# Spreading 500 samples of an edge list over the partitions: by a matmul from the list in SBUF in place of a DMA of single words

## The chip, the cores and the metric

The kernel runs on one core of a Trainium2 chip. The metric is the device time of one execution in microseconds (us), and the median of three runs is given. Beside it there is one profiled execution, from which all views of the trace are taken. Engines are named as the profile names them: PE (TensorE), DVE (VectorE), ACT (ScalarE), POOL (GpSimd) and SP (SyncE). A "q" behind the name (ACTq, SPq) marks what an engine's sequencer does, such as issuing a DMA.

## The reference

A graph has 3,125 nodes with 128 features each and 100,000 edges. The edge list is given as `src`, `dst` and `edge_type_8` (0 to 7), sorted by `dst`. Four graph layers follow one another; each adds its result to its input, and a layer norm follows. Cut to what matters:

```
edge_index = stack([src, dst])
x = layernorm(x + L0(x, ..., src, dst))             # three GCN layers, weights by degree, self loops
x = layernorm(x + L1(x, edge_index, W, b))          # sum over the neighbours and the node itself
x = layernorm(x + L2(x, edge_index, eps, ...))      # GIN: sum over neighbours, two linear layers with batch norm
x = layernorm(x + L3(x, edge_index, edge_type_8, ...))   # two relational layers, a mean per relation
```

Every layer needs the adjacency of the graph, which the kernel has to make out of the edge list first.

## The kernel before, in words

The function `listed` does the work (a second function, `general`, is there for graphs that don't fit the first one's limits, and does not run here). It has three parts.

**From the edge list to matrices.** The three lists are loaded as tiles of 125 partitions by 800 words (L171). Two arrays go back to DRAM from them: `dsf`, which is the target list as floats in rows of 200 (written at L182, made by the cast at L181), and `pk`, in which target, type and source of an edge are packed in one word (written at L189, made by two DVE operations at L184 and L186; L190 writes a short tail of -1 behind it). Then each half block of 64 nodes needs the place where its edges begin. `search(s)` finds it for two half blocks at a time, for 128 slots in parallel. First it counts how many of 500 samples of the target list, every 200th edge, lie below the node's number (L213); the samples must lie in every partition for that (`smb`). The count gives the row of `dsf` that an indirect DMA of POOL fetches (`g`, L220); counting in that row (L225) gives the exact place, `ptr`. `keys(s)` fetches the edges from there out of `pk` (`ew`, L235), unpacks them, transposes them on PE and leaves them in `kT`. `total(b)` makes one-hot matrices of them on DVE (L162), multiplies them on PE (L272) to a 128-row slab of the adjacency, and writes the slab and its transpose to DRAM. These calls are made for `s` from 0 to 12, two calls of `search` ahead.

**The layers L0 to L2** multiply with the adjacency slabs. Between their matmuls the generator `relations()` makes matrices for the eight relations.

**The relational layers L3** multiply with these, and gather the edges of the last blocks by indirect DMAs of POOL.

How the 500 samples come to lie in every partition is the subject of this document. `smp` is loaded by a DMA on ACT's queue that takes every 200th word of `dst` in DRAM (L174); `smf` is its cast to float on DVE (L179); a matmul with a row of ones (L193) spreads the row over 128 partitions in PSUM, and ACT copies it to `smb` (L195):

```python
nc.scalar.dma_start(smp, p["dst"].rearrange("(o i j) -> o i j", o=1, j=200)[:, :, 0])
...
nc.tensor.matmul(t[:, :500], ones[0:1, :], smf, start=True, stop=True)
```

What is issued in which order is not the order of the source. A scheduler places each engine's instructions by what they depend on, and moves loads that depend on nothing to the front. So ACT's queue also holds, near the start, the load of the node features `xa` (L473, 24 blocks of 128 rows, and L476, the last 53 rows) and eight loads of bias and scale columns by `column` (L95), which only layers L2 and L3 use. DMAs from SP and ACT report their end on eight semaphores, which the scheduler hands out in turn: the ninth DMA waits, before it is issued, for the end of the first, and so on. In the built program the waits of the start stand as follows. The column loads are the tenth to the seventeenth of these DMAs. On ACT the order is `smp`, `xa`, a load of the activation table, the copy to `smb`, the rest of `xa`, and then the eight column loads, which wait in turn for `e_dst`, `xa`, `e_src`, `e_edge_type`, `dsf`, `pk<-none`, the rest of `xa`, and `pk<-w`. On SP the order is `e_dst`, `e_src`, `e_edge_type`, `dsf`, `pk<-none`, `pk<-w`. On DVE it is some memsets, `smf`, `df`, `w`, `w` with the target, two copies for `iota50`, `identb`, and then the first counts of `search(0)`.

Of the kernel before, what the change touches and what calls it, by code (L numbers as in the profile page):

```python
# [8 lines left out]
F32 = mybir.dt.float32  # L9
BF = mybir.dt.bfloat16  # L10
I32 = mybir.dt.int32
# [4 lines left out]
OP = mybir.AluOpType  # L16
# [14 lines left out]
EP = 125  # L31
# [14 lines left out]
def cols(m0, nb):  # L46
    return slice(m0 * P, (m0 + nb) * P)
# [25 lines left out]
def listed(ctx: ExitStack, tc: tile.TileContext, p: dict, out: bass.AP, bad):  # L73


    nc = tc.nc
# [4 lines left out]
    ident = const.tile([P, P], F32, name="ident")  # L81
# [5 lines left out]
    ones = const.tile([P, P], F32, name="ones")  # L87
# [60 lines left out]
    with tc.tile_pool(name="f_bg", bufs=1) as bg, tc.tile_pool(  # L148
        name="f_ps", bufs=1, space=PSUM
# [17 lines left out]
        with tc.tile_pool(name="f_t1", bufs=1) as t1:  # L167

            ei = [t1.tile([EP, ET], I32, name=f"e_{n}") for n in ("dst", "src", "edge_type_8")]
            for t, name in zip(ei, ("dst", "src", "edge_type_8")):  # L170
                nc.sync.dma_start(t, p[name].rearrange("(p t) -> p t", p=EP))  # L171
            smp = t1.tile([1, 500], I32, name="smp")
            with nc.allow_non_contiguous_dma(reason="every 200th edge"):
                nc.scalar.dma_start(smp, p["dst"].rearrange("(o i j) -> o i j", o=1, j=200)[:, :, 0])  # L174
            nid = t1.tile([P, NC2], F32, name="nid")
            nc.gpsimd.iota(nid, pattern=[[2 * P, SB], [1, 2]], base=0, channel_multiplier=2,
                           allow_small_or_imprecise_dtypes=True)
            smf = t1.tile([1, 500], F32, name="smf")
            nc.vector.tensor_copy(smf, smp)  # L179
            df = t1.tile([EP, ET], F32, name="df")  # L180
            nc.vector.tensor_copy(df, ei[0])  # L181
            nc.sync.dma_start(dsf.rearrange("(p a) c -> p (a c)", p=EP), df)  # L182
            w = t1.tile([EP, ET], I32, name="w0")
            nc.vector.scalar_tensor_tensor(w, ei[2], 12, ei[1], op0=OP.logical_shift_left, op1=OP.bitwise_or)  # L184
            w2 = t1.tile([EP, ET], I32, name="w1")
# [4 lines left out]
            nc.sync.dma_start(pk[E:].rearrange("(o t) c -> o (t c)", o=GM), none)  # L190

            t = psum.tile([P, 512], F32, name="mi", tag="mi", bufs=2)
            nc.tensor.matmul(t[:, :500], ones[0:1, :], smf, start=True, stop=True)  # L193
            smb = t1.tile([P, 500], F32, name="smb")
            nc.scalar.copy(smb, t[:, :500])  # L195

# [110 lines left out]
            for g in range(2):  # L307
                t = psum.tile([P, 512], F32, name="mi", tag="mi", bufs=2)
                rs = t1.tile([P, 512], F32, name="rs", bufs=2)
                nc.vector.memset(rs, 0.0)  # L310
                for i in range(4 * g, min(7, 4 * g + 4)):
                    q, w = 32 * (i % 4), min(512, NP - 512 * i)
# [19 lines left out]
            t = psum.tile([P, 512], F32, name="mi", tag="mi", bufs=2)  # L332
# [5 lines left out]
            t = psum.tile([P, 512], F32, name="mi", tag="mi", bufs=2)  # L338
# [132 lines left out]
        with tc.tile_pool(name="f_nd", bufs=1) as nd:  # L471
# [127 lines left out]
            t = psum.tile([P, 512], F32, name="mi", tag="mi", bufs=2)  # L599
# [69 lines left out]
            for m0, nb in CH:  # L669
                t = psum.tile([P, 512], F32, name="bld", tag="bld", bufs=2)  # L670
                for i in range(nb):
                    o = t[:, cols(i, 1)]
# [8 lines left out]
    with tc.tile_pool(name="f_rel", bufs=1) as rp, tc.tile_pool(  # L681
        name="f_psr", bufs=1, space=PSUM
# [175 lines left out]
        with tc.tile_pool(name="f_hr", bufs=1) as hp:  # L858
# [15 lines left out]
            for m0, nb in CH:  # L874
                o = psum.tile([P, 512], F32, name="mi", tag="mi", bufs=2)
                for a in range(2):
                    nc.tensor.matmul(o[:, : nb * P], root2[:, a, :], hT[:, a, cols(m0, nb)],
                                     start=(a == 0), stop=(a == 1))
# [623 lines left out]
@with_exitstack  # L1502
def gnn_kernel(ctx: ExitStack, tc: tile.TileContext, p: dict, out: bass.AP):
    bad = ctx.enter_context(tc.tile_pool(name="flag", bufs=1)).tile([P, 1], I32, name="bad")
    listed(tc, p, out, bad)
    rv = tc.nc.values_load(bad[0:1, 0:1], min_val=0, max_val=1)  # L1506
    with tc.If(rv > 0):
        general(tc, p, out)
# [32 lines left out]
```

## Time and profile before

| | |
|---|---|
| median of 3 runs | 2260.39 us (2258.17 to 2264.78) |
| the profiled execution's own time | 2260.0 us |
| its span, first to last instruction | 2258.2 us |
| mean granted TensorE clock | 0.938 of full speed |
| PE busy, DVE busy, POOL busy, ACT busy | 1955.4, 1376.9, 954.5, 791.5 us |
| DMA, mean over the span | 192 GB/s |
| first 30 us: PE, DVE, ACT busy | 2.03, 7.59, 2.02 us |
| 30 to 58 us: PE, DVE busy | 9.42, 22.05 us |
| 58 to 263 us (adjacency slabs): PE, DVE busy | 138.39, 175.09 us |
| 330 to 960 us (L0 to L2): PE busy | 624.17 us of 630 |

The span leaves out 1.8 us of the execution's own time. The rows of the table with a stretch of time are answers of the trace for that stretch: in the first 30 us no engine is busy for more than a quarter of the time, so it is waits that set its length; after that DVE, and later PE, carry the kernel.

### The profile page before, as it was taken

The page shows a single profiled execution, that of the slowest core. Times are in us where ns is not written, and L with a number is a line of the kernel's source. Part 1 is how long each engine was busy: PE and PEld are TensorE (multiplying, and loading weights), DVE is VectorE, ACT ScalarE, POOL GpSimd, SP SyncE. Part 2 cuts the span into 40 slices and gives each one's busy share as a digit, 9 for nine tenths or more (in the row PEclk, how much of TensorE's full clock was granted, in tenths as well). Part 3 has the DMA queues.
Part 4 walks back from the last instruction along what each step waited for, and adds up shares of the span by engine and source line. Part 5 has one row for each costly group of instructions (what it writes and reads, how often), then busy time and mean ns, then how long its engine had stood idle before and what let it go on. Part 6 is the DMA issues. An engine that isn't in the chain of part 4 may idle for free. (4 is left out here: it accounts for less than half of the span.)

```text
span 2258.2 us, 32584 instructions
## 1 busy us (share of the span) xinstructions
PE 1955.4 (87%) x12551; PEld 1351.3 (60%) x12551; DVE 1376.9 (61%) x2385; ACT 791.5 (35%) x1027; POOL 954.5 (42%) x898
## 2 busy tenths in 40 slices
PE   1666669999999999957999999999878998899894
PEld 1444436666665555445668667758745776777772
DVE  4888889999996430045435345435337776666663
ACT  1666734545442110044223233233224333232230
POOL 3222121211210000002757547727723887777875
PEclk9777779999999999978999999999989999999996
DMA  3444476887888666427657467637637887788762
GB/s 93 176 189 166 178 193 211 287 284 257 272 277 269 180 193 177 120 60 222 173 140 212 139 185 213 187 117 207 172 99 219 241 238 221 201 229 228 199 172 77
DMA packets 384638, 433.10 MB, mean 192 GB/s; under 512 B 28731, under 2 KB 350301, under 8 KB 384472
## 3 DMA queue, kind: packets, MB, share of 16 engines
q1 hardware_dynamic: 314318, 278.95, 40.7%
q0 software_dynamic: 45920, 119.66, 18.2%
q10 hardware_dynamic: 24234, 32.31, 5.0%
q8 instruction: 100, 1.64, 0.3%
q14 instruction: 66, 0.54, 0.1%
HBM read 319.22 MB, written 111.58 MB: 191 GB/s over the span
## 5 line engine op out<-in xcount | busy, mean ns | idle before, releaser
L738 PE MATMUL acc<-m,hilo 128*128 128x384 f32 (+1 forms) x3200 | 758.5, 383 | 12.0 <-DVE m L735 6.6
L772 POOL DMA_INDIRECT gx<-xt_d,gsrc x355 | 393.6, 1109 | 573.2 <-DMA m<-rel 357.2
L738 PEld LDWEIGHTS acc<-m,hilo 128*128 128x128 f32 x3200 | 577.6, 193 | 80.3 <-issue 8.9
L539 PE MATMUL acc<-m,parts 128*128 128x512 bf16 (+1 forms) x2625 | 539.3, 357 | 15.7 <-issue 12.7
L772 POOL DMA_INDIRECT gx<-ht_d,gsrc x355 | 412.9, 1163 | 167.0 <-issue 56.4
L733 ACT CAST m<-m 128x1920 fp32r<-128x1920 uint8 (+1 forms) x128 | 264.2, 2064 | 540.1 <-PE acc L738 491.5
L735 DVE CAST m<-m 128x2560 fp32r<-128x2560 uint8 (+1 forms) x192 | 302.6, 1576 | 161.3 <-PE acc L738 92.5
L539 PEld LDWEIGHTS <-parts 128*128 128x128 bf16 x2625 | 255.3, 98 | 238.3 <-issue 17.9
L780 PE MATMUL ga<-oh,gx 128*128 128x192 bf16 (+1 forms) x2442 | 273.5, 246 | 98.8 <-DMA gx<-ht_d,gsrc 57.7
L780 PEld LDWEIGHTS <-gx 128*128 128x128 bf16 x2442 | 170.7, 99 | 206.9 <-DMA gx<-ht_d,gsrc 83.1
L456 ACT CAST rb<-bld 128x800 uint16<-128x800 f32 x179 | 143.9, 828 | 129.7 <-PE bld L449 121.4
L463 POOL DMA_DIRECT2D rel<-rb x112 | 64.3, 582 | 287.5 <-ACT rb L456 162.6
L764 DVE TENSOR_TENSOR oh<-iota,gkey 128x768 bf16<-128x768 bf16 (+1 forms) x188 | 99.5, 530 | 92.2 <-PE ga L780 89.2
L162 DVE TENSOR_TENSOR lo<-iota,kT 128x2048 bf16<-128x2048 bf16 x100 | 122.0, 1220 | 0.0
L712 DVE TENSOR_TENSOR e<-mi,t 128x512 f32<-128x512 f32 x50 | 34.3, 688 | 133.8 <-ACT t L711 133.8
L272 PE MATMUL bld<-hi,lo 128*128 128x50 bf16 x1600 | 74.4, 200 | 46.1 <-DVE hi L162 38.9
L449 PE MATMUL bld<-rhq,rlo 128*128 128x200 bf16 x896 | 107.6, 252 | 1.8 <-DVE rb L458 1.1
L272 PEld LDWEIGHTS <-lo 128*128 128x128 bf16 x1600 | 63.4, 107 | 70.6 <-DVE hi L162 26.3
L449 PEld LDWEIGHTS <-rlo 128*128 128x128 bf16 x896 | 82.4, 98 | 36.7 <-issue 9.0
L162 DVE TENSOR_TENSOR rhq<-iota,kT 128x3200 bf16<-128x3200 bf16 x56 | 102.2, 1824 | 0.0
L828 PE MATMUL mi<-wr,hT 128*128 128x512 f32 x200 | 93.9, 604 | 4.8 <-DVE e L712 4.7
L285 ACT ACTIVATE av<-mi 128x896 bf16<-128x896 bf16 (+1 forms) x100 | 82.8, 835 | 31.4 <-PE mi L284 30.1
(212 smaller groups left out, 1813.4 us busy)
## 6 DMA issues: line engine op xcount, KB each, us to landing
m<-rel SPq DMA_DIRECT2D x160, 320.0 KB, 4.1
rel<-rb POOLq DMA_DIRECT2D x112, 400.0 KB, 6.5
m<-adj SPq DMA_DIRECT2D x60, 640.0 KB, 7.3
m<-rel SPq DMA_DIRECT2D x160, 240.0 KB, 3.2
m<-adj_t SPq DMA_DIRECT2D x40, 640.0 KB, 4.1
m<-adj SPq DMA_DIRECT2D x45, 480.0 KB, 6.1
adj_t<-at SPq DMA_DIRECT2D x25, 800.0 KB
adj<-av SPq DMA_DIRECT2D x25, 800.0 KB, 3.3
```

The lines of the kernel that those rows point to most:

```text
L162: nc.vector.tensor_tensor(o, (iota2 if of is None else of)[:, None, :width, :].to_broadcast([P, PU // 2, width, 2]), k[:, :, None, :].to_b ...
L272: nc.tensor.matmul(pt[:, j, : 2 * NB], lo[:, j // 2, :, j % 2], hi[:, j // 2, :, j % 2], start=True, stop=True)
L449: nc.tensor.matmul(pt[:, k, : R * NB], lo[:, j // 2, :, j % 2], hq[:, j // 2, :, j % 2], start=True, stop=True)
L456: nc.scalar.copy(o, src)
L539: nc.tensor.matmul(o, x[:, k, :], m(k - k0), start=(k == 0 and i == 0), stop=last and more is None)
L733: nc.scalar.copy(v, src)
L735: nc.vector.tensor_copy(v, src)
L738: nc.tensor.matmul(acc[:, :w], x[:, 5 * g + k, :], m[:, k, :w], start=(g == 0 and k == 0 and i == 0), stop=(g == 4 and k == 4 and i == 1),)
L764: nc.vector.tensor_tensor(oh[:, : nt // 2], iota2[:, None, : GW * R, :].to_broadcast([P, nt // 2, GW * R, 2]), gkey[:, g, t : t + nt].rear ...
L772: nc.gpsimd.indirect_dma_start(out=gx.rearrange("p i c -> p (i c)"), out_offset=None, in_=table[:], in_offset=bass.IndirectOffsetOnAxis(ap ...
L780: nc.tensor.matmul(acc[:, a:z], gx[:, i, :], oh[:, t % 4 // 2, a - c0 : z - c0, t % 2], start=(a // 512 not in seen), stop=(t == GT[g] - 1 ...
L828: nc.tensor.matmul(o, hT[:, a, cols(b, 1)], wr[:, a, r : r + 4, :].rearrange("p r c -> p (r c)"), start=(a == 0), stop=(a == 1))
```

## The change

The DMA of 500 single words and its cast are gone. The sources are loaded on ACT's queue in place of SP's. The samples are taken from the float list `df`, which lies in SBUF: partition p holds edges 800p to 800p+799, so columns 0, 200, 400 and 600 of the 125 partitions are the 500 samples. Each of these columns is multiplied into the identity (four DVE operations of 125 by 125), and a matmul of ones over 125 partitions leaves all 500 samples in every partition. Their order differs, which the count does not see.

```diff
             ei = [t1.tile([EP, ET], I32, name=f"e_{n}") for n in ("dst", "src", "edge_type_8")]
-            for t, name in zip(ei, ("dst", "src", "edge_type_8")):
-                nc.sync.dma_start(t, p[name].rearrange("(p t) -> p t", p=EP))
-            smp = t1.tile([1, 500], I32, name="smp")
-            with nc.allow_non_contiguous_dma(reason="every 200th edge"):
-                nc.scalar.dma_start(smp, p["dst"].rearrange("(o i j) -> o i j", o=1, j=200)[:, :, 0])
+            for t, name, q in zip(ei, ("dst", "src", "edge_type_8"), (nc.sync, nc.scalar, nc.sync)):
+                q.dma_start(t, p[name].rearrange("(p t) -> p t", p=EP))
...
-            smf = t1.tile([1, 500], F32, name="smf")
-            nc.vector.tensor_copy(smf, smp)
             df = t1.tile([EP, ET], F32, name="df")
             nc.vector.tensor_copy(df, ei[0])
             nc.sync.dma_start(dsf.rearrange("(p a) c -> p (a c)", p=EP), df)
+
+            smf = t1.tile([EP, 4, EP], F32, name="smf")
+            for j in range(4):
+                nc.vector.tensor_scalar(smf[:, j], ident[:EP, :EP], df[:, 200 * j : 200 * j + 1], None,
+                                        op0=OP.mult)
...
-            nc.tensor.matmul(t[:, :500], ones[0:1, :], smf, start=True, stop=True)
+            nc.tensor.matmul(t[:, :500], ones[:EP, :], smf.rearrange("p j q -> p (j q)"), start=True, stop=True)
```

The scheduler's order changes with it. One DMA fewer is issued at the start, so the column loads are the ninth to the sixteenth. On ACT the built program now has `e_src`, `xa`, the rest of `xa`, the eight column loads, then the activation table and the copy to `smb`; the column loads wait in turn for `e_src`, `e_dst`, `xa`, `e_edge_type`, `pk<-none`, `dsf`, the rest of `xa`, and `pk<-w`. On SP it is `e_dst`, `e_edge_type`, `pk<-none`, `dsf`, `pk<-w`. On DVE `df` leads, then `w`, `w` with the target, `iota50`, `identb`, the four operations for `smf`, two operations for a later stage (`gw`), and the counts of `search(0)`. Behind that the order of every engine is the same as before.

## The prediction

> **What bounds the kernel now.** The change touches the first 30 us alone, so I ask two things: does a delay or a gain there reach the end, and what sets the length of that stretch. For the first: the table of stretches has DVE busy for 7.59 us of the first 30 and for 175.09 of the 205 us from 58 to 263. All that DVE and PE do after 30 us hangs on the first rows of `g` and the words `ew` fetched from there, in a fixed order. A shift of the start shifts the whole, one for one.
>
> For the second, the timeline of 0 to 33 us (start, duration, engine, line, and in brackets the idle time before it and what ended it):
>
> ```profile
> 0.74 1.38 ACTq L174 DMA_DIRECT2D smp<-in_dst  x1
> 3.21 1.28 ACT L195 ACT_TABLE_LOAD   x1 [0.90 <-issue]
> 15.43 0.41 DVE L179 CAST smf<-smp 1x500 f32<-1x500 int32 x1 [12.67 <-DMA smp<-in_dst]
> 15.89 2.03 PE L193 MATMUL mi<-smf,ones 1*128 1x500 f32 x2 [15.89 <-DVE smf L179]
> 17.95 0.57 ACT L195 COPY smb<-mi 128x500 f32<-128x500 f32 x1 [13.46 <-PE mi L193]
> 20.99 0.16 DVE L217 CAST irow<-crow 128x2 int32<-128x2 f32 x1
> 25.06 1.11 POOL L220 DMA_INDIRECT g<-dsf,irow  x1 [20.02 <-DMA dsf<-df]
> 28.22 0.91 ACTq L95 DMA_DIRECT2D c_L_gnn_b<-in_L_gnn_b  x2
> 30.13 0.42 DVE L225 TENSOR_SCALAR_CACHE_REDUCE junk<-g,nid 128x200 bf16<-128x200 f32 x1
> ```
>
> The wait of 12.67 us for `smp` looks like the prize. But `smf` also stood at the head of DVE, ahead of `df`, and `irow` was ready at 21.15: POOL started only at 25.06, on the landing of `dsf`. Of the words' delay nothing is on the path except that it held `df` back. The row at 28.22 shows the last two column loads on ACT; the last one waits for `pk<-w`. The trace's semaphore records give the landings: `e_dst` 7.9, `e_src` 12.6, `smp` 15.4, `e_edge_type` 16.2, `xa` 20.9, `dsf` 24.2, rest of `xa` 28.2, `pk<-w` 28.4 us.
>
> What sets these landings is in the answers on DMA for short stretches. The first block is 13 to 14 us, the second 16 to 20, the third 20.5 to 23 (queue, packets, MB, share of 16 engines; q1 is SP's, q10 ACT's):
>
> ```profile
> q1 hardware_dynamic: 38, 0.12, 30.4%
> q10 hardware_dynamic: 38, 0.00, 2.1%
> ```
> ```profile
> q10 hardware_dynamic: 282, 0.38, 34.1%
> ```
> ```profile
> q1 hardware_dynamic: 98, 0.31, 31.4%
> q10 hardware_dynamic: 230, 0.00, 4.6%
> ```
>
> SP's queue never takes more than 31%, which is 5 engines of 16: every transfer of 125 partitions goes through the same five. In the second block `dsf`, issued at 16.35, doesn't move while `xa` (also 5 engines' worth by then) drains. These five engines are full from 3 to 27 us without a gap. The start is bound by them.
>
> **What the Trainium skill says.** In "DMA: Bandwidth & Descriptors", section "Why a DMA increments its semaphore by 16 and not by 1", the number of engines of a transfer is the largest number up to 16 that divides its slowest dimension, and from SP or ACT the lowest-numbered engines are taken: 5 for 125 partitions, 10 for 500 words. The trace agrees (30.4% and 31.4%; of the words one half landed by 5.5 us, the other, on the five busy engines, at 15.1 to 15.4). The same page, "Issuing engines are not separate DMA queues", says that a second issuing queue saves issue time alone. Section "Queues, rings and completion order" says that an engine takes the queues' packets in turn; the first block agrees, 38 words beside 38 list packets.
>
> **The change part by part.**
>
> 1. *The 500 words go.* With 38 words between them the lists ran at 38 packets per us (first block), and at 40 per us beside 182 words from 3.5 to 4.25 us; without words it is 39 (third block). I take the saving on the five engines as nothing; the other bound is 250 words on five engines in the 9 us in which the list ran at 27 packets per us instead of 38, which would be 2.5 us. I ascribe that slowness to `xa`, which ran on the other eleven engines at just that time.
> 2. *`e_src` on ACT's queue.* Same five engines, same bytes. It saves 0.3 us of SP's issuing. `e_dst` and `e_src` now alternate, so `e_dst` comes later: 25 packets are through by 3.3 us as before, then 27 per us while `xa` runs on the other eleven engines (8 us, 216), and the last of 250 at 11.6; with 0.4 to land, 12 us instead of 7.9. `xa` is issued about 1 us earlier, as 500 words took 1.38 us to issue and 125 rows 0.40: its clash with the lists ends 1 us earlier, worth 1 us x (38-27)/38 = 0.3 us of drain.
> 3. *`df` no longer waits for `smp`.* It starts at 12, not 15.8, `dsf` is issued at 12.6. It gains little, as its packets come behind `e_edge_type` (25 packets per engine, alternating with `xa`: 25 x 0.24 us from 11.6, done at 17.6) and `xa`. `w` starts at 18.0 and `pk<-w` is issued at 20.2, while the five engines are still busy with `xa` and `dsf`. So no gap opens, and the drain of the five ends where it did, less 0.3, and less some 0.2 for POOL's first fetch, which was on the same engines at 27 us and is now later. **`pk<-w` lands at 27.9** (24.9 when the words cost their 2.5; 29.5 when the alternation costs what I don't see).
> 4. *Four DVE operations for `smf`.* The nearest row is the one-scalar-pair operation of 128x128 floats at L137, 0.34 us: at most 1.4 us together, against 0.41 for the cast. Behind `w`, `w`, `iota50` (0.36) and `identb` (0.23) they end at 22. The matmul over 125 rows in place of one takes as many columns: 2.03 us, done at 24. (Nothing here shows a float matmul of this shape at that time; 1 us less or 2 more stays under the cover named next.)
> 5. *ACT's order, which the diff doesn't show.* The copy to `smb` now stands behind eight column loads, and the last of them waits for `pk<-w`. ACT therefore reaches the copy at 27.9 + 0.48 (issue of the last load: 0.91 for two) + 1.28 (table load, formerly idle time at 3.21) + 0.57 (copy) + 0.1 of gaps = 30.3. The table load has lost its cover. Items 1 to 4 are covered by this wait up to 29.7.
> 6. *From there.* Two counts, `crow` and `irow` took 18.76 to 21.15, of which two `gw` operations between them took 0.4, and these are now ahead: 2.0, so 32.3. POOL starts 0.27 after an `irow` of its own (41.44 to 41.71), or 0.6 later still, as it did at 25.06 after the landing at 24.2: 32.6 to 33.2. The second row of `g` starts 1.42 later and is read 2.63 after its start (34.78 to 37.41, undisturbed): 36.6 to 37.2. It was read at 30.13.
>
> Sum: +6.5 to +7.1, I take **+6.8 us**. Before, POOL waited on `dsf`; now it waits on ACT, which waits for `pk<-w`, which lands 3.7 us after `dsf` did, and 5 us of ACT, DVE and POOL come behind it. Next late after the stall at `smb` is the second `ew`, as before. On the profiled execution's 2260.0 this gives 2266.8; its median of the runs shown is 0.4 above, so 2267.2.
>
> **The rivals.**
>
> *Likeliest: the column loads hold `smb`, the drain is as long as before.* +6.8, from +5.0 to +8.5 as `pk<-w` lands between 26.2 and 29.6. Chance 0.56.
>
> *The drain shortens (the other side).* The words and the clash cost the list what item 1 grants them; `pk<-w` lands at 24.9 and the shift is 36.9 - 30.13 - 3.0 = +3.7: no measurable difference. It decides when `pk<-w` lands before 27.9. For it: 27 packets per us against 38 while words were there; against: 38 beside words in the first block. Chance 0.19.
>
> *The drain lengthens.* `e_edge_type` and `dsf` share with `xa` packet by packet; if `e_edge_type` lands at 21, `pk<-w` is issued at 23.2, the five engines stand empty for 2 us and it lands at 30: +9. Chance 0.19.
>
> *The change does what it says, without the wait on ACT.* Were the copy free at 24, POOL would start at 26.9 and the read come at 30.8: +0.7. The built order speaks against it. Chance 0.05. A real gain of 0.3% would need POOL at 18, before the lists are in; I leave 0.01.
>
> **How the numbers follow.** A measurement of this kernel can tell about 0.3%, 6.8 us, from no change, and the forecast lies on this bound. Of the likeliest case a little over half (0.33) lies above it, and so does the lengthened drain but for 0.01 (0.18): slower 0.51. Within the bound are the rest of the likeliest (0.23), the shortened drain (0.19), that 0.01 and most of the last case (0.04): same 0.47. Faster 0.02. The three runs shown spread from 2258.2 to 2264.8, so a median may be off by 3 us: the range runs from +3.7 less 3 to +9 plus 3, which is 2261 to 2272.
>
> **What would show it.** Right: the copy to `smb` starts at about 29.7, after the last column load and the table load; POOL's first `g` near 33 waits on DVE, not on a DMA; `g`'s second read near 37; from there every stretch has its old length. Step 3 is wrong if the last column load is issued before 26 or after 30. Step 5 is wrong if the copy follows the matmul at 24. The whole is wrong if the kernel's time moves by other than the second read's shift.

## The result and the profile after

| | before | after |
|---|---|---|
| median of 15 runs each, us | 2260.35 (2257.5 to 2264.78) | 2267.46 (2259.14 to 2271.28) |
| profiled execution: own time, span, us | 2260.0, 2258.2 | 2267.88, 2266.1 |
| mean granted clock | 0.938 | 0.939 |

The ratio of after to before is 1.0028, with a 95% interval from 1.0017 to 1.0038: the change costs 6.3 us, at least 3.8 and at most 8.6. 2267.2 was forecast. The interval leaves out 1, so the change makes the kernel slower; the ratio is just under the 0.3% that the prediction named as its bound.

The timeline of the changed kernel's first 36 us answers to the one shown of the kernel before (start, duration, engine, line, and in brackets the idle time ahead and what ended it):

```profile
2.74 13.21 ACTq L476 DMA_DIRECT2D xa<-in_x  x1
12.12 0.58 DVE L176 CAST df<-e_dst 125x800 f32<-125x800 int32 x1 [9.36 <-DMA e_dst<-in_dst]
18.00 0.99 DVE L184 SCALAR_TENSOR_TENSOR w<-e_edge_type,e_src 125x800 int32<-125x800 int32 x1 [5.30 <-DMA e_edge_type<-in_edge_type]
20.45 0.86 DVE L181 TENSOR_SCALAR smf<-ident,df 125x125 f32<-125x125 f32 x4
21.36 2.04 PE L193 MATMUL mi<-smf,ones 125*128 125x500 f32 x2 [21.36 <-DVE smf L181]
26.15 1.65 ACTq L95 DMA_DIRECT2D c_L_gnn_b<-in_L_gnn_b  x2
27.84 1.28 ACT L195 ACT_TABLE_LOAD   x1 [26.32 <-DMA c_L_gnn_b<-in_L_gnn_b]
29.13 0.58 ACT L195 COPY smb<-mi 128x500 f32<-128x500 f32 x1
31.84 1.11 POOL L220 DMA_INDIRECT g<-dsf,irow  x1 [26.80 <-DVE irow L217]
35.90 0.42 DVE L225 TENSOR_SCALAR_CACHE_REDUCE junk<-g,nid 128x200 bf16<-128x200 f32 x1 [0.83 <-DMA g<-dsf,irow]
```

Read it from the bottom. The second row of `g` is read at 35.90 where it was 30.13: +5.77 us. POOL's first fetch now waits for `irow`, on DVE; before, it waited for the landing of `dsf`. `irow` waits for the copy to `smb` at 29.13. The matmul that makes the samples had ended at 23.40, so its result lay in PSUM for 5.7 us. What ended ACT's idle time of 26.32 us is the last of the column loads; by the trace's records it was issued at 27.46, released by the landing of `pk<-w` at 27.44. (The row at 26.15 merges the last two loads with the wait between them.) The table load of 1.28 us, which stood at 3.21 under idle time, follows.

The waits of the same stretch (engine and line, what was waited for, total, times, longest) say it in two rows:

```profile
POOL g L220 <- DVE irow L217: 26.8, 1, 26.8
ACT L195 <- DMA c_L_gnn_b<-in_L_gnn_b: 26.3, 1, 26.3
```

One warning about reading shifts later in the trace. The 51st of the 100 slab operations `lo` starts at 174.5 us in place of 168.6, +5.9; the first operation of the stage behind, `rlo`, is at +3.7; the spans differ by 7.9. Single executions wander by some us in the slab stage and in L3, so the start is compared trace by trace, and the whole only by medians.

### The profile page after: what moved, and what is told of

The parts are those of the page before. It is cut to its first block, busy times and chain, and to the rows that moved or that the text cites. A ratio compares the mean times of both kernels' runs of the same rounds, so it can differ in the third digit from the quotient of the medians.

```text
span 2266.1 us, 32552 instructions
## 1 busy us (share of the span) xinstructions
PE 1954.2 (86%) x12519; PEld 1349.1 (60%) x12551; DVE 1377.5 (61%) x2388; ACT 791.9 (35%) x1027; POOL 962.6 (42%) x898
## 4 chain that ended last, share of the span: by engine, by line
PE 53%; DMA 20%; DVE 13%; issue 6%; ACT 4%; POOL 3%; ACTq 0%; POOLq 0%; DVEq 0%; SPq 0%
PE acc L738 18%; PE acc L539 17%; DMA gx<-ht_d,gsrc 8%; PE ga L780 5%; DMA gx<-xt_d,gsrc 5%; PE mi L818 4%; PE mi L828 3%; PE bld L449 2%; POOL gx L772 2%; DVE lo L162 2%; DMA g<-dsf,irow 2%; DVE hi L162 1%; DVE rhq L162 1%; DMA back<-ht_d 1%; PE mi L555 1%
## 5 line engine op out<-in xcount | busy, mean ns | idle before, releaser
L539 PE MATMUL acc<-m,parts 128*128 128x512 bf16 (+1 forms) x2593 | 533.8, 357 | 16.6 <-issue 12.6
L772 POOL DMA_INDIRECT gx<-ht_d,gsrc x355 | 421.8, 1188 | 163.4 <-issue 60.9
L449 PEld LDWEIGHTS <-rlo 128*128 128x128 bf16 x896 | 82.5, 98 | 36.6 <-issue 9.0
```

The lines of the kernel that those rows point to most:

```text
L449: nc.tensor.matmul(pt[:, k, : R * NB], lo[:, j // 2, :, j % 2], hq[:, j // 2, :, j % 2], start=True, stop=True)
L539: nc.tensor.matmul(o, x[:, k, :], m(k - k0), start=(k == 0 and i == 0), stop=last and more is None)
L772: nc.gpsimd.indirect_dma_start(out=gx.rearrange("p i c -> p (i c)"), out_offset=None, in_=table[:], in_offset=bass.IndirectOffsetOnAxis(ap ...
```

## The experiments

The theory: the cost is **ACT's order**, a copy that everything waits for behind loads that nobody needs yet. The rivals: the new way to the samples is itself longer; or the second queue lengthens the drain of the five DMA engines. The measure of the start is always the second read of `g`: 30.13 before, 35.90 after. The experiments ran in two sets, each on a chip of its own with its own runs of the kernel before; "ratio" is to those. On the second set's chip all times are some 70 us longer: its median for the kernel before is 2330.04 us, and in the traces taken there the extra time lies in L3. So its times stand against that alone. The ratios are the recorded ones. They lie up to 0.16% from the quotients of the plain medians (0.9938 against 0.9954 for the sixteen engines below), so a difference of that size is not read from them.

### The copy moved to DVE

```diff
-            nc.scalar.copy(smb, t[:, :500])
+            nc.vector.tensor_copy(smb, t[:, :500])
```

> The changed kernel with one edit: the copy from PSUM to smb is made by DVE, not ACT, so it no longer stands behind the eight column loads. Theory 1 (ACT's order is the cost): DVE copies when the matmul ends, at 23.4 us; smb is there at 24.1, irow at 26.2, POOL's first g starts at 26.5 on DVE's word, and the second row of g is read at 30.5 to 31.3 us, against 35.9 in the changed kernel and 30.1 before. The time is 2261, 5 to 6 us under the changed kernel and within 1 us of the kernel before. Theory 2 (the new way of making the samples is itself longer, as it waits for the edge types and two packing operations): the second read stays near 36 and the time near 2267. Theory 3 (the second queue lengthens the drain of the five engines): the same as theory 2.

Ratio 0.9999 (0.9985 to 1.0013), after's being 1.0028. Its timeline:

```profile
23.28 0.68 DVE L195 COPY smb<-mi 128x500 f32<-128x500 f32 x1 [1.21 <-PE mi L193]
26.10 1.11 POOL L220 DMA_INDIRECT g<-dsf,irow  x1 [21.06 <-DMA c_L_gnn_beta<-in_L_gnn_beta]
28.50 1.28 ACT L256 ACT_TABLE_LOAD   x1 [26.98 <-DMA c_L_gnn_g<-in_L_gnn_g]
30.42 0.42 DVE L225 TENSOR_SCALAR_CACHE_REDUCE junk<-g,nid 128x200 bf16<-128x200 f32 x1 [1.17 <-DMA g<-dsf,irow]
```

The copy follows the matmul at once and the second read is at 30.42, 0.3 us off the kernel before. (What the brackets name behind POOL's fetch, here a column load, is only what came last by the profile's records. `irow` was ready at 25.80, and POOL started 0.30 us later, as it did behind `irow` in the changed kernel.) The table load still comes at 28.50, behind the column loads: ACT's queue is held as long as in the changed kernel, and now nobody waits for it. At the start this one edit takes back all of the cost but 0.3 us. So the drain with two queues and the longer way to the samples cost at most that there. The time agrees less sharply: its interval reaches from 3.4 us under the kernel before to 2.9 over it.

### The column loads moved to SP

```diff
-            nc.scalar.dma_start(t, p[name].rearrange("(n p) -> p n", p=P))
+            nc.sync.dma_start(t, p[name].rearrange("(n p) -> p n", p=P))
```

> The changed kernel with one edit: the eight column loads are issued from SP's queue, so nothing stands ahead of the copy to smb on ACT but the loads of e_src and xa; the copy stays on ACT. In the built order the rest of xa now waits for xa itself, which landed at 22.8 in the changed kernel. Theory 1 (the column loads ahead of the copy are the cost): the table load starts at about 23.1, the copy at 24.4, the second row of g is read at 31 to 32 us against 35.9, and the time is 4 to 5 us under the changed kernel. Rival (the copy on ACT is late for another cause, the blocked issue of the rest of xa or the table load alone): the copy stays near 29, and so do the second read (36) and the time (7 us over the kernel before).

The other way round: the copy stays on ACT and what stood ahead of it goes.

```profile
21.04 1.28 ACT L195 ACT_TABLE_LOAD   x1 [19.52 <-DVE gw L407]
22.66 0.57 ACT L195 COPY smb<-mi 128x500 f32<-128x500 f32 x1 [0.34 <-PE mi L193]
29.47 0.42 DVE L225 TENSOR_SCALAR_CACHE_REDUCE junk<-g,nid 128x200 bf16<-128x200 f32 x1 [0.81 <-DMA g<-dsf,irow]
```

The copy waits for PE alone, and the second read is at 29.47, earlier than the 31 to 32 that I expected, since the rest of `xa` was issued at 20.8 and not at 23. Ratio 0.9995 (0.9973 to 1.0017): after's 1.0028 is not in it, but the two intervals meet at 1.0017, so it is the trace that decides. The edit also brought the lists in somewhat earlier (edge types at 17.1, 17.9 after), and the matmul started 0.8 us earlier; the copy started 6.5 us earlier. The rest, 5.7 us, is the time for which the result had lain in PSUM. What this edit and the copy on DVE have in common is that the copy no longer stands behind the column loads.

### The queue alone

The kernel before, with the sources on ACT's queue and the samples still by 500 words:

```diff
-            for t, name in zip(ei, ("dst", "src", "edge_type_8")):
-                nc.sync.dma_start(t, p[name].rearrange("(p t) -> p t", p=EP))
+            for t, name, q in zip(ei, ("dst", "src", "edge_type_8"), (nc.sync, nc.scalar, nc.sync)):
+                q.dma_start(t, p[name].rearrange("(p t) -> p t", p=EP))
```

> The kernel before with one half of the change: the sources are loaded on ACT's queue, the samples still come by the DMA of 500 words. The built order keeps the copy to smb ahead of the column loads. Theory 1: nothing holds the copy; the words come behind e_src, smb is there at about 19, dsf lands between 22 and 23.5, POOL's first g starts at 22.5 to 24.5 and the second read is at 27 to 29.5 us: 1 to 3 us earlier than before, time 2257 to 2260. Theory 3 (the second queue lengthens the drain): second read at 33 or later, time 2264 or more.

```profile
11.19 0.58 DVE L181 CAST df<-e_dst 125x800 f32<-125x800 int32 x1 [8.43 <-DMA e_dst<-in_dst]
18.57 0.58 ACT L195 COPY smb<-mi 128x500 f32<-128x500 f32 x1 [13.64 <-PE mi L193]
22.53 1.11 POOL L220 DMA_INDIRECT g<-dsf,irow  x1 [17.49 <-DMA dsf<-df]
28.69 0.42 DVE L225 TENSOR_SCALAR_CACHE_REDUCE junk<-g,nid 128x200 bf16<-128x200 f32 x1
```

Here the scheduler keeps the copy ahead of the column loads. It also puts `df` ahead of `smf` on DVE: `df` was made at 11.19 in place of 15.76 and `dsf` issued at 11.79 in place of 16.35. So this is not the queue quite alone. The start is 1.4 us shorter (28.69): `dsf` landed at 21.6 in place of 24.2, and POOL started 2.5 us earlier, of which its fetches gave back one. They ran beside the rest of `xa` and `pk<-w`, which may be why. Ratio 0.9999 (0.9983 to 1.0014): a gain of 1.4 us lies within the interval and is not shown by the time. The rival of a longer drain is out. Nor do the words show a cost: with them on the five engines `pk<-w` landed at 26.5, no later than without them (27.4). That is one trace each, with `xa` issued at different times (2.78 and 1.55), so it speaks against a cost of 2.5 us and not against one of some tenths.

### The matmul alone

The changed kernel with all lists on SP:

```diff
-            for t, name, q in zip(ei, ("dst", "src", "edge_type_8"), (nc.sync, nc.scalar, nc.sync)):
+            for t, name, q in zip(ei, ("dst", "src", "edge_type_8"), (nc.sync, nc.sync, nc.sync)):
```

> The changed kernel with all three lists on SP's queue: the other half alone. The copy to smb stands behind the column loads here too, but with the completion semaphores handed out in another turn they wait for xa, the three lists, the rest of xa and the short tail of pk, not for dsf or pk<-w. Theory 1: the copy starts when the matmul ends or the rest of xa has landed, at 22 to 24 us, the second read is at 30 to 32, and the time is 2260 to 2263. Theory 2 (the new way of making the samples is itself longer): second read at 35 to 37, time 2266 to 2268, as in the changed kernel.

```profile
22.87 2.04 PE L193 MATMUL mi<-smf,ones 125*128 125x500 f32 x2 [22.87 <-DVE smf L181]
23.75 0.34 ACTq L95 DMA_DIRECT2D c_L_gnn_beta<-in_L_gnn_beta  x1
24.13 2.75 ACTq L95 DMA_DIRECT2D c_L_gnn_b<-in_L_gnn_b  x2
26.91 1.28 ACT L195 ACT_TABLE_LOAD   x1 [26.16 <-DMA c_L_gnn_beta<-in_L_gnn_beta]
28.20 0.57 ACT L195 COPY smb<-mi 128x500 f32<-128x500 f32 x1
34.86 0.42 DVE L225 TENSOR_SCALAR_CACHE_REDUCE junk<-g,nid 128x200 bf16<-128x200 f32 x1 [0.69 <-DMA g<-dsf,irow]
```

My number was wrong: I expected the copy at 22 to 24, and it came at 28.20, the second read at 34.86 (+4.7), ratio 1.0018 (1.0002 to 1.0033). That is next to the number of the rival, a longer way to the samples (35 to 37), but the copy shows that it is not the rival's cause: the matmul ended at 24.91, and the copy stood behind the column loads and the table load for 3.3 us more. I had seen that here no column load waits for `pk<-w`, and taken that for freedom. But the sixth waited for the rest of `xa`, until 23.75, and the last two took 2.75 us to issue. The matmul, too, ended later than in the changed kernel (23.40), as the edge types landed at 19.4. So the copy can be late without a wait for `pk<-w`; other waits and slow issues of the loads ahead of it were enough here. The matmul and its order carry the cost (+4.7), the queue alone none (-1.4); the parts don't add to +5.8, as each changes what the last column load waits for.

### Sixteen engines for the lists

As the kernel with the copy on DVE, but with the lists as 80 partitions of 1250, in which the Trainium skill ("DMA: Bandwidth & Descriptors", section "Why a DMA increments its semaphore by 16 and not by 1") has 16 engines for a transfer. There are 400 samples in place of 500 then, rows of `dsf` have 250 words in place of 200, and the packing is done in place:

```diff
+    EP, ET, RW = 80, 1250, 250
...
-    dsf = dram.tile([E // 200, 200], F32, name="dsf")
+    dsf = dram.tile([E // RW, RW], F32, name="dsf")
...
-            smf = t1.tile([EP, 4, EP], F32, name="smf")
-            for j in range(4):
+            smf = t1.tile([EP, 5, EP], F32, name="smf")
+            for j in range(5):
...
-            w = t1.tile([EP, ET], I32, name="w0")
+            w = ei[2]
...
-            w2 = t1.tile([EP, ET], I32, name="w1")
+            w2 = ei[1]
...
```

> The copy on DVE as in e1, and the lists as 80 partitions of 1250 in place of 125 of 800 (samples every 250th edge, 400 of them, rows of dsf of 250; the packing is done in place to save SBUF), so that their transfers go through 16 engines in place of five. If the five engines bind the start: the lists are in at about 10 us in place of 17.9, the matmul ends at about 16, POOL's first g starts at about 18.7 and the second read is near 23, 7 us earlier than before; time 2253, all of it kept to the end. If not the engines but the DMA rate of the core binds the lists: second read near 30, time about 2260, as in e1.

The DMA of 3 to 8 us (queue, packets, MB, share of 16 engines), and its timeline:

```profile
q10 hardware_dynamic: 240, 0.65, 50.9%
q1 hardware_dynamic: 193, 0.66, 50.0%
```
```profile
12.14 1.70 PE L194 MATMUL mi<-smf,ones 80*128 80x400 f32 x2 [12.14 <-DVE smf L182]
13.88 0.57 DVE L196 COPY smb<-mi 128x400 f32<-128x400 f32 x1 [0.47 <-PE mi L194]
16.38 1.11 POOL L221 DMA_INDIRECT g<-dsf,irow  x1 [11.34 <-DMA c_L_gnn_g<-in_L_gnn_g]
20.51 0.47 DVE L226 TENSOR_SCALAR_CACHE_REDUCE junk<-g,nid 128x250 bf16<-128x250 f32 x1 [0.86 <-DMA g<-dsf,irow]
```

The trace agrees with the sixteen engines: the two queues together fill all of them, and the semaphore of `e_dst` counts sixteen landings in place of five. SP's queue takes 50%, where in no stretch of 1 us of the kernel before it took more than 34.1%. The edge types land at 8.0 us (16.2 before, 17.9 after), and the second read is at 20.51, 9.6 us earlier than before and 2.5 earlier than I expected, as the lists were in at 8.0 and not at 10. Ratio 0.9938 (0.9918 to 0.9958), which is 9.5 to 18.5 us; by the plain medians it is 10.3. The start gives 9.6; the 26 counts of samples take 15.4 us in all in place of 18.1 and the 26 in the rows 12.2 in place of 10.8, at most another 1.3. The five engines bound the start, as the prediction said, and this version beats both kernels.

With the copy back on ACT:

> As e5_sixteen_engines, but the copy to smb is ACT's again. Theory 1: the column loads still hold it. Their last issue ended at 16.7 in e5, so the table load and the copy take until 18.6, against 14.5 on DVE: the second row of g is read at 24.5 to 25, 4 us later than in e5 (20.5), and the time is 4 us longer than e5's, 0.25 to 0.5% under the kernel before. Rival (with fast transfers ACT's order costs nothing): second read at 20.5 to 21.5 and the time of e5.

```profile
16.70 1.28 ACT L196 ACT_TABLE_LOAD   x1 [15.34 <-DMA c_L_gnn_beta<-in_L_gnn_beta]
18.00 0.49 ACT L196 COPY smb<-mi 128x400 f32<-128x400 f32 x1
24.54 0.47 DVE L226 TENSOR_SCALAR_CACHE_REDUCE junk<-g,nid 128x250 bf16<-128x250 f32 x1 [0.80 <-DMA g<-dsf,irow]
```

The second read is at 24.54, 4.0 us later, as expected: the order on ACT costs with fast transfers too. The ratio, 0.9938 (0.9915 to 0.9961) on its own chip, is that of the sixteen engines with the copy on DVE on another, so the time does not show these 4 us; intervals of 0.2% on each side could hide them. One thing does not fit: against the kernel before, the start gives 5.6 us here and the counts at most 1.3, 6.9 in all, but the interval begins at 9.1 (12.7 by the plain medians). Where the rest was gained is not shown.

### The features later

Two kernels hold the load of `xa` back until the packed list is made, the first on top of the copy on DVE, the second on top of the sixteen engines:

```diff
+            nc.vector.tensor_copy(xa[:EP, 0, 0:1], w2[:, 0:1])
```

> The copy on DVE as in e1_copy_on_dve, and the load of xa held back until the packed list is made (a copy of one column of it into xa, which the load then overwrites). If the drain of the five engines sets the start: without xa between them e_dst and e_src land at about 10 us, e_edge_type at 13, pk<-w at 20 to 22; the matmul ends at 19, POOL's first g starts at 22 and the second read is at 26 to 27, as xa now runs beside the fetches of g: 3 to 4 us earlier than before and than e1, time 0.1 to 0.2% under the kernel before. If the lists' own rate sets it, xa or not: second read near 30, as in e1.

> e5_sixteen_engines with the load of xa held back as in e6. On 16 engines xa and the lists share 220 GB/s, so without xa e_edge_type lands at about 7 in place of 8.0, and all behind it moves by 1 us; xa then runs at 10 to 18 us, beside dsf and pk<-w, and its end meets the first fetches of g at 16 to 19. I expect the second read at 19.5 to 21 (20.5 in e5) and a time within 2 us of e5's: with sixteen engines the order of the loads is worth little, as DVE's and PE's own steps set the length. Rival (the drain still binds): second read at 17 to 18, 3 us under e5.

The first, around its first fetch:

```profile
17.47 2.04 PE L194 MATMUL mi<-smf,ones 125*128 125x500 f32 x2 [17.47 <-DVE smf L181]
22.36 1.11 POOL L221 DMA_INDIRECT g<-dsf,irow  x1 [17.32 <-DMA pk<-w]
27.70 0.42 DVE L226 TENSOR_SCALAR_CACHE_REDUCE junk<-g,nid 128x200 bf16<-128x200 f32 x1 [5.63 <-DMA g<-dsf,irow]
28.04 0.42 DVE L226 TENSOR_SCALAR_CACHE_REDUCE junk<-g,nid 128x200 bf16<-128x200 f32 x1
```

Without `xa` beside them the lists are in 4 us earlier (`w` at 13.9, 18.0 after), the matmul ends at 19.5 and POOL starts at 22.36, as forecast. But the fetch then takes 5.3 us to be read in place of 2.7 (26.10 to 28.82 with the copy on DVE alone), while `xa` now runs beside it. The second read comes at 28.04, against 26 to 27 expected; ratio 0.9991 (0.9974 to 1.0007), no difference shown. The second kernel:

```profile
21.49 0.47 DVE L227 TENSOR_SCALAR_CACHE_REDUCE junk<-g,nid 128x250 bf16<-128x250 f32 x1
```

It reads 1.0 us later than with the sixteen engines alone, a little outside what I expected; ratio 0.9956 (0.9937 to 0.9976). In both kernels the transfer that was moved out of one stretch ran in the next, beside the fetches; with sixteen engines there was nothing to win.

## Why the prediction was right, step by step

In the changed kernel, too, the two queues share little more than five engines' worth (31%), here from 16 to 20 us:

```profile
q10 hardware_dynamic: 311, 0.23, 17.6%
q1 hardware_dynamic: 111, 0.24, 16.9%
```

- *What bounds the start, and that it shifts the rest.* Right. The share above is as it was before, and the kernel with sixteen engines shows the bound directly. That SP's queue "never takes more than 31%" was put too sharply: from 5 to 6 us it took 34.1%. "One for one" agrees with after (+5.8 at the start, 3.8 to 8.6 in the time) and with the sixteen engines; runs of this spread cannot show it closer than some 3 us, and the sixteen engines with the copy on ACT gained more than the start explains.
- *Steps 1 to 3, the drain.* `e_dst` landed at 12.1 (12 forecast), `e_edge_type` at 17.9 (17.9 to 18.0), `pk<-w` was issued at 20.0 (20.2) and landed at 27.44 (27.9). The rival of a shorter drain, with its 24.9, and that of a longer one, with 30, are both out. The drain ended 1.0 us earlier than before, not 0.5, and its terms are not borne out one by one: the part of `xa` on the other eleven engines landed at 13.0 before and 13.1 after, so the clash with the lists did not end earlier. Why the drain is shorter stays open, and with it whether a second queue saves issuing time alone. By the semaphore records four of the five engines had written their part of `pk<-w` by 26.45, and ACT waited for the fifth alone.
- *Step 4.* Four operations took 0.86 us (at most 1.4), the matmul 2.04 (2.03), and it ended at 23.40 (24). The bound from L137 was high by a factor of 1.6.
- *Step 5, the step that decides.* Shown by two opposite edits. Copy at 29.13 (about 29.7), done at 29.71 (30.3). `pk<-w` had landed 0.5 us earlier than forecast, and the last load took 0.34 us to issue in place of 0.48.
- *Step 6.* `irow` at 31.55 (32.3), POOL at 31.84 (32.6 to 33.2): the extra 0.6 us of POOL's start, seen once before, did not come back. Second read at 35.90 (36.6 to 37.2).
- *The size.* The start moved by 5.77, not by 6.5 to 7.1: terms of 0.5 in the landing, 0.3 in the issue and the counts, and up to 0.6 in POOL's start were each taken too large. That the time's 7.1 us by medians (6.3 by the ratio) meets the forecast of 6.8 is partly luck; the difference to 5.8 is within the interval.
- *Two sums of the rivals.* The 24.9 of the shorter drain is 3.0 us under 27.9, where step 1 grants the words 2.5. With the copy free at 24 the steps named (26.9, then 1.42 and 2.63) give 30.95, not 30.8. The forecast rests on neither.
- *The chances.* A ratio of 1.0028 is on the bound of 0.3% where I had split them, 0.51 to 0.47. The measurement was finer than I took it to be, about 0.1% to each side.
- *What was not seen.* Issuing the rest of `xa` held ACT's queue for 13.2 us, and the first column load for 2.2. It did no harm in the changed kernel only because the waits behind it ended later.

## What to carry to other kernels

Read the order that the scheduler made, on every engine, and not the diff: a change of loads can put a copy that everything waits for behind other instructions of its engine, and it can change which earlier transfers these wait for, as completion semaphores are handed out in turn. (Why the scheduler moved the copy here is not shown.) An engine that has nothing to do is no free place for such a copy while its queue also issues loads that wait. And before a wait is removed, ask what bounds the transfers behind it: here it was five engines of sixteen, set by 125 partitions, and 80 partitions gave more than either way to the samples.

## What the runs showed of the hardware that I had not expected

Issuing a DMA can itself take long. The 53 rows of `xa` (L476) took 0.28 us to issue at 17.96 in the kernel before; issued at 2.74, right behind the 24 blocks of `xa` on the same queue, they took 13.21 us, 13.33 with the copy on DVE, and 6.95 with sixteen engines for the lists. The engine's own instructions wait behind such an issue. It does not wait until `xa` has landed: in the changed kernel the issue ended at 15.95 and `xa` landed at 22.8, with the matmul alone the two are at 11.63 and 18.7, and in the kernel before the short issue at 17.96 also came 3 us ahead of `xa`'s landing. So it looks as if only so much of one queue may still be outstanding when the next is issued; how much is not shown. In the changed kernel this cost nothing. In the kernel with the matmul alone one of the last two column loads took 2.23 us to issue (0.39 in the kernel before and in the changed one), perhaps for the same reason, and the copy to `smb` stood behind it.
